# Layer 1: the store of the upper four chunks of image 13 as nine accesses of every ninth partition

## The chip, the cores and the metric

The kernel runs on one core of one Trainium2 chip. The metric is the time of one execution on the device in microseconds (us); the median of several runs counts. Names used below: PE is TensorE, DVE is VectorE, ACT is ScalarE, POOL is GpSimd, SP is SyncE, the engine that issues most DMAs here. A core has sixteen DMA engines. "Landing" is the moment at which the last of the sixteen marks of a DMA has been counted on its semaphore.

## The reference

Input and output are 16 images of 128 channels by 64 by 64, float32. Layer 0 adds to `x` a diagonal LSTM of its group-normalised self; layer 1 adds a small simulated quantum circuit, again of the group-normalised input. Cut to what matters:

```python
def _L0_conv_ref(x, w_is, b_is, w_ss, b_ss):      # skewed rows, a scan over 127 columns
    i_s = einsum('oi,bihw->bohw', w_is, skew(x)) + b_is
    def step(carry, ist):
        gates = ist + w_ss[:, :, 0] @ shifted(h) + w_ss[:, :, 1] @ h + b_ss
        c_new = f * c + i * g
        h_new = o * tanh(c_new)
    return unskew(hs)

def _L1_conv_ref(x, pre_w, pre_b, q_weights, post_w, post_b):
    xq = x.transpose(0, 2, 3, 1).reshape(-1, C) @ pre_w.T + pre_b
    z = _simulate(xq, q_weights)                  # 4 qubits, 2 layers
    out = z @ post_w.T + post_b
    return out.reshape(N, H, W, -1).transpose(0, 3, 1, 2)

x = x + _L0_conv_ref(_gn(x), ...)
x = x + _L1_conv_ref(_gn(x), ...)
```

## The kernel before, in words

The 128 channels lie on the 128 partitions. The whole activation is kept on the chip as far as it fits: the tile `ring` holds 40 of the 64 image rows of all 16 images; the other 24 rows of each image, `low`, lie in DRAM.

Three stages follow each other. Stage one loads `x`, takes its statistics and prepares weights (to about 90 us). Stage two is the scan, a chain of steps on PE, DVE, ACT and POOL (to about 1276 us); it hardly uses DMAs. Stage three is layer 1, and the change lies at its end.

In stage three an image is cut into eight chunks of 512 positions (`CHUNK`), `k` = 0 to 7. Chunks 0 to 2 come from `low` by way of small tiles (`spare`, `trio`, `low`), loaded by POOL's queue (`load`, `low_rows`); chunks 3 to 7 are read in `ring`. For each image: `angles` (line 1099, PE) makes the angles, `sines` (ACT, DVE) their sines, `squares` (line 1129, PE, then ACT) the amplitudes, `outputs` (line 1149, PE) the values, and `finish` adds them to the image on DVE, one instruction for each chunk (line 1167), and issues the store (line 1173) on SP. The loop at the end runs over images 1 to 15 and works them in order; an order written out by hand overlaps neighbours (all inside `tc.manual_schedule()`).

How the stores are cut: `together(b, k)` tells how many chunks go into one store. Chunks 0 to 3 go out singly, 256 KB each: a row of 2 KB on each of 128 partitions. Of chunks 4 to 7, images 1 to 3 make two stores of 512 KB, images 4 to 14 one store of 1 MB (a row of 8 KB on each partition), issued when chunk 7 is done. Image 15, the last, stores all its chunks singly. So images 4 to 14 have five stores each, image 15 has eight.

The order on SP is the order of the program. Each DMA that SP issues takes the next of eight semaphores in turn, and first waits until the DMA that used that semaphore before, eight places earlier, has landed. It waits for DVE's instruction of its chunk as well. At most eight of SP's stores are so under way at any time. The end of the program (line 1290) waits until every store has landed.

Of the kernel before, what the change touches and what calls it, by code (L numbers as in the profile page):

```python
# [17 lines left out]
NB = 16  # L18
# [13 lines left out]
FEW = 96  # L32
TWICE = 128
LEAST = 128
AHEAD = RING - SLOTS
BAND = NW + 1
NSTEP = BAND + NW + SLOTS - 1
# [45 lines left out]
def kernel(  # L83
# [16 lines left out]
    nc = tc.nc  # L100
# [38 lines left out]
    def place(r):  # L139

        return (r + AHEAD if r < SLOTS else r - SLOTS) * NW

# [21 lines left out]
    with ExitStack() as scan:  # L164
# [55 lines left out]
        def above(v, a, b):  # L220

            v = v[:, 1, 0:1]
            dims = [list(v.ap[0]), [NB - NC, 2], [1, b - a]]
            return bass.AP(v.tensor, v.offset + a - NB, dims)
# [8 lines left out]
        with ExitStack() as prep:  # L233
# [25 lines left out]
            def rows(b):  # L259
                half = SLOTS // 2  # L260
                first = 0 if b else AHEAD
                early = ((first, half - first), (half, half))
                for r, n in (*(early if b < 3 else ((0, SLOTS),)), (SLOTS, AHEAD)):
                    nc.sync.dma_start(
# [6 lines left out]
            def behind(b):  # L271
# [10 lines left out]
                out=qw, in_=q_weights.rearrange("l w a -> (l w a)").partition_broadcast(P)  # L282
            )
            nc.sync.dma_start(out=ring[:, 0, place(0) : place(AHEAD)], in_=xv[0, :, 0 : AHEAD * NW])
            for i in range(2):
# [146 lines left out]
            def cleared():  # L432
                for v in (*hst, *xns, none, cst[:, :, 0:LEAST]):
                    nc.gpsimd.memset(v, 0.0)
                    yield
                nc.gpsimd.memset(eps, EPS)
                nc.gpsimd.tensor_sub(apart_of, ident, group)
                yield
                nc.gpsimd.memset(w_image, 0.0)
                yield  # L440
# [60 lines left out]
            for g in ORDER:  # L501
                first[g] = ps_gate.tile([P, 2, NC], F32, name=f"ps0_{g}", tag="gate")
                for w, rhs in ((w1T, hst[0][:, :, 0 : LEAST // 2]), (w0T, above(hst[0], 0, LEAST // 2))):
                    nc.tensor.matmul(
                        first[g][:, :, 0 : LEAST // 2],
                        lhsT=w[:, g * 128 : (g + 1) * 128],
# [106 lines left out]
        def reach(t):  # L613

            b = columns(t)[1]
            return b + 4 if b < NC else b

        def plain(t):
            a, b = columns(t)
            return b - a <= FEW  # L620
# [5 lines left out]

        def wide(t, least=LEAST):

            a, b = columns(t)[0], reach(t)
            return max(0, min(a, b - least)), max(b, min(NC, a + least))  # L630

        def diagonal(t, band, q, j0, j1):


            r = 2 * j0 + q + AHEAD * (1 - band)
            at = r * NW + t - BAND * band - 2 * j0 - q
# [15 lines left out]
        def apart(op, *groups):  # L652

            for key in groups:
                tc.declare_no_dep(op.ins, group=key, reason="other rows of the ring")
            return op

        def ahead_of(op, band, j1):

            apart(op, "stores", *(f"reload{g}" for g in reloads if band == 0 or 2 * j1 <= AHEAD + 4 * g))  # L660

# [24 lines left out]
        def gate_ps(t):  # L686

            a, b = wide(t, LEAST // 2)
            ps = {} if t else first
# [172 lines left out]
        def step(t, ps):  # L862

            a, b = columns(t)
            few = plain(t)
            a0, b0 = wide(t, LEAST // 2 if few else LEAST)
            w = reach(t)
# [209 lines left out]
    def rows_of(b, k):  # L1077
        if k < NT:
            return lows[NT * b + k]
        at = place(2 * ROWS * k)  # L1080
        return ring[:, b, at : at + CHUNK]

    def half(v, c):

        if c is None:
            return v
        return v[:, c * BLOCK : (c + 1) * BLOCK]
# [71 lines left out]
    def finish(b, h, po, c=None):  # L1159
        for j in range(4):  # L1160
            k = 4 * h + j
            v = rows_of(b, k)
            x1, y, o = half(v, c), po[j], ov[b, :, k * CHUNK : (k + 1) * CHUNK]
            to = v
            if c is not None:
                o, to = o[:, c * BLOCK : (c + 1) * BLOCK], x1
            nc.vector.scalar_tensor_tensor(to, y, b_out, x1, ALU.add, ALU.add)  # L1167
            n = together(b, k) if c is None else 1
            if (k + 1) % n == 0:
                if n > 1:  # L1170
                    at = place(2 * ROWS * (k + 1 - n))
                    o, to = (u[:, at0 : at0 + n * CHUNK] for u, at0 in ((ov[b], (k + 1 - n) * CHUNK), (ring[:, b], at)))
                nc.sync.dma_start(out=o, in_=to)
            if c is None or c == 1 and k < NT:
                places.append(v)

    def together(b, k):

        if k < 4 or b == NB - 1:
            return 1  # L1180
        return 2 if b < 4 else 4
# [8 lines left out]
    with tc.manual_schedule():  # L1190
# [15 lines left out]
        angles(1, 1, th, (1,))  # L1206
        ths[1, None] = th
        finish(0, 0, po, 0)
        squares(0, 1)
        po = outputs(0, 1, 0)  # L1210
        finish(0, 1, po, 0)
        later = sines(1)
        next(later)
        po = outputs(0, 0, 1, (0, 1))
        th = angles(2, parts=(0,))
        po += outputs(0, 0, 1, (2, 3))
        finish(0, 0, po, 1)
        next(later, None)
        po = outputs(0, 1, 1, (0,))
# [74 lines left out]
```

## Time and profile before

| | us |
|---|---|
| median of 3 runs (lowest, highest) | 1399.43 (1399.15, 1399.73) |
| the profiled execution's own time | 1399.66 |
| its span, first to last instruction | 1397.8 |

The stages, by windows of the profile (busy us in each):

| window, us | PE | DVE | ACT | POOL | DMA share | GB/s |
|---|---|---|---|---|---|---|
| 0 to 88, loads and statistics | 68.25 | 76.01 | 60.23 | 27.12 | 0.98 | 392 |
| 88 to 1276, the scan | 1174.74 | 795.28 | 685.97 | 840.14 | 0.07 | 24 |
| 1276 to 1397.8, layer 1 | 108.03 | 102.30 | 40.09 | 25.39 | 0.93 | 360 |
| of it 1345 to 1387 | 39.59 | 40.74 | 12.41 | 0.00 | 1.03 | 412 |
| of it 1387 to 1397.8 | 0.00 | 0.00 | 0.00 | 0.00 | 0.59 | 227 |

How to read it: the DMA share is the mean busy share of the sixteen DMA engines (a little over 1 where packets overlap). The stores of layer 1 in the profile's list of issues, with size and median time from issue to landing:

```profile
out_dram<-ring SPq DMA_DIRECT2D x11, 1024.0 KB, 9.1
out_dram<-ring SPq DMA_DIRECT2D x37, 256.0 KB, 7.2
out_dram<-low SPq DMA_DIRECT2D x14, 256.0 KB, 9.1
```

SP's stream is shown in rows of its own (SPq): start, duration, line, what is stored, and how many in a row. The first of the eleven stores of 1 MB is image 4's, the tenth image 13's, the eleventh image 14's.

### The profile page before, as it was taken

To read this page: it belongs to the slowest core of one execution; us is meant where nothing else is said; L and a number is where in the kernel's file an instruction comes from. 1 tells how busy PE (TensorE), PEld (TensorE's weight loads), DVE (VectorE), ACT (ScalarE), POOL (GpSimd) and SP (SyncE) were. 2 spreads that over 40 slices of the span, in tenths; PEclk is the share of its full clock that TensorE was granted. 3 is DMA by queue.
4 is the path that set the end of the run, shared out by engine and by line. 5 is a ranking of instruction groups with operands and counts; after the bars stand their busy time and mean duration, and the time that the engine had idled before them with its cause. 6 is when DMAs were issued, how large, how long until landed. Compare 5 with 4: busy or idle time off the path is not lost. (4 is left out here: it accounts for less than half of the span.)

```text
span 1397.8 us, 19939 instructions
## 1 busy us (share of the span) xinstructions
PE 1351.0 (97%) x6058; PEld 966.6 (69%) x6058; DVE 973.6 (70%) x2520; ACT 786.3 (56%) x1881; POOL 892.6 (64%) x1584
## 2 busy tenths in 40 slices
PE   7789999999999999999999999999999999989996
PEld 6668887777777777767777767777777778886332
DVE  6973565577767775677777776666665566876996
ACT  6765666555555555555555555555555566644331
POOL 3236777766677777777777766777777667764400
PEclk9999999999999999999999999999999999999998
DMA  9940000000000000133333100000000000014998
GB/s 373 417 199 1 2 1 1 1 1 1 1 1 1 1 1 1 60 121 121 121 121 120 61 1 1 1 1 0 1 1 1 1 0 1 1 31 144 382 415 354
DMA packets 52746, 107.02 MB, mean 77 GB/s; under 512 B 3824, under 2 KB 31504, under 8 KB 49568
## 3 DMA queue, kind: packets, MB, share of 16 engines
q1 hardware_dynamic: 49024, 95.17, 18.3%
q0 software_dynamic: 3472, 10.58, 2.0%
q8 instruction: 48, 0.79, 0.2%
q14 instruction: 58, 0.48, 0.1%
q10 hardware_dynamic: 144, 0.01, 0.0%
HBM read 59.61 MB, written 46.14 MB: 76 GB/s over the span
## 5 line engine op out<-in xcount | busy, mean ns | idle before, releaser
L693 PE MATMUL ps<-spare,wxT 128*128 128x512 f32 (+18 forms) x1280 | 479.6, 518 | 0.6 <-POOL spare L684 0.6
L887 DVE TENSOR_TENSOR ps<-ps,both 128x256 f32<-128x256 f32 (+9 forms) x536 | 219.8, 410 | 295.5 <-PE ps L872 291.1
L891 ACT ACTIVATE ps<-ps,bias 128x512 f32<-128x512 f32 (+23 forms) x480 | 279.2, 583 | 219.5 <-DVE ps L887 183.1
L693 PEld LDWEIGHTS ps<-spare,wxT 128*128 128x128 f32 x1280 | 230.9, 190 | 173.2 <-issue 155.5
L872 PE MATMUL ps<-trio,w1T 128*128 128x256 f32 (+14 forms) x1088 | 306.3, 363 | 0.0
L872 PE MATMUL ps<-trio,w0T 128*128 128x256 f32 (+14 forms) x1088 | 305.5, 362 | 0.0
L922 ACT COPY both<-ps 128x256 f32<-128x256 f32 (+9 forms) x536 | 189.6, 356 | 181.0 <-PE ps L872 161.5
L872 PEld LDWEIGHTS ps<-spare,wsT 128*128 128x128 f32 x1088 | 196.0, 190 | 78.8 <-DVE spare L957 30.4
L872 PE MATMUL ps<-spare,wsT 128*128 128x256 f32 (+14 forms) x1088 | 243.6, 365 | 1.6 <-DVE spare L957 1.3
L730 POOL TENSOR_TENSOR ring<-ring,spare 128x256 f32<-128x256 f32 (+15 forms) x375 | 231.4, 643 | 18.3 <-DVE spare L957 18.0
L872 PEld LDWEIGHTS ps<-trio,w1T 128*128 128x128 f32 x1088 | 201.6, 190 | 22.3
L872 PEld LDWEIGHTS ps<-trio,w0T 128*128 128x128 f32 x1088 | 201.1, 190 | 21.2
L684 POOL TENSOR_TENSOR spare<-spare,rstd 128x512 f32<-128x512 f32 (+10 forms) x160 | 170.9, 1068 | 14.2 <-DVE rstd L528 1.7
L678 POOL TENSOR_TENSOR spare<-ring 128x256 f32<-128x256 f32 (+13 forms) x165 | 139.4, 845 | 0.0
L951 ACT ACTIVATE g<-cst 128x256 f32<-128x256 f32 (+20 forms) x320 | 103.0, 368 | 64.2 <-DVE cst L950 63.6
L957 DVE TENSOR_TENSOR spare<-g,ps 128x256 f32<-128x256 f32 (+17 forms) x319 | 105.3, 367 | 44.3 <-ACT g L951 39.4
L720 POOL TENSOR_TENSOR trio<-spare 128x240 f32<-128x240 f32 (+9 forms) x136 | 102.5, 754 | 36.7 <-DVE spare L957 33.1
L672 POOL TENSOR_TENSOR spare<-ring,mean 128x256 f32<-128x256 f32 (+15 forms) x191 | 122.5, 641 | 2.5 <-DVE mean L517 2.0
L891 ACT ACTIVATE g<-ps,bias 128x512 f32<-128x512 f32 (+20 forms) x160 | 97.3, 608 | 27.6 <-DVE ps L887 21.3
L950 DVE TENSOR_TENSOR cst<-cst,ps 128x256 f32<-128x256 f32 (+20 forms) x320 | 104.5, 368 | 5.5
L947 DVE TENSOR_TENSOR ps<-ps,g 128x512 f32<-128x512 f32 (+20 forms) x160 | 95.1, 594 | 18.7 <-ACT g L891 18.5
L939 DVE TENSOR_TENSOR cst<-cst,ps 128x512 f32<-128x512 f32 (+20 forms) x160 | 92.7, 579 | 16.5 <-POOL spare L231 10.9
(385 smaller groups left out, 1172.3 us busy)
## 6 DMA issues: line engine op xcount, KB each, us to landing
ring<-in_x_dram SPq DMA_DIRECT2D x13, 1024.0 KB, 9.8
low<-ring SPq DMA_DIRECT2D x6, 2048.0 KB, 7.6
ring<-in_x_dram SPq DMA_DIRECT2D x6, 2048.0 KB, 8.2
out_dram<-ring SPq DMA_DIRECT2D x11, 1024.0 KB, 9.1
out_dram<-ring SPq DMA_DIRECT2D x37, 256.0 KB, 7.2
trio<-in_x_dram SPq DMA_DIRECT2D x7, 768.0 KB, 7.6
rest<-in_x_dram SPq DMA_DIRECT2D x7, 768.0 KB, 7.8
ring<-in_x_dram SPq DMA_DIRECT2D x18, 256.0 KB, 9.9
```

Source lines behind the costliest of these rows:

```text
L672: op = nc.gpsimd.tensor_sub(by_pairs(xn, 0, j0, j1), x0, over(mean1, j1 - j0))
L678: op = nc.gpsimd.tensor_sub(by_pairs(xn, 1, j0, j1), lower, of)
L684: nc.gpsimd.tensor_mul(v, v, r)
L693: nc.tensor.matmul(ps[g][:, :, a:b], lhsT=wxT[:, g * 128 : (g + 1) * 128], rhs=xns[t % 2][:, :, a:b], start=t > 0, stop=True, skip_group_c ...
L730: op = engine.tensor_add(x1, x1, by_pairs(new, q, j0, j1))
L872: nc.tensor.matmul(out, lhsT=w[:, g * 128 : (g + 1) * 128], rhs=rhs, start=False, stop=True, skip_group_check=True,)
L887: nc.vector.tensor_add(v, v, both[g][:, a:b])
L891: nc.scalar.activation(to[:, :, a:w], ps[g][:, :, a:w], FUNC[g], bias=bias[:, g : g + 1])
L922: nc.scalar.copy(both[g][:, a:b], ps[g][:, 0, a:b])
L950: nc.vector.tensor_add(c[:, q], c[:, q], ig[:, q])
L951: nc.scalar.activation(th[:, q, a:w], c[:, q], AF.Tanh)
L957: nc.vector.tensor_mul(new[:, q, a:v], th[:, q, a:v], act[GO][:, q, a:v])
```

## The change

In `finish`, when the store of several chunks of image 13 (`b == NB - 3`) is due, it is issued as nine DMAs in place of one. DMA number p takes the partitions p, p + 9, p + 18 and so on: 15 partitions for p = 0 and 1, 14 for p = 2 to 8, each with its whole row of 8 KB. All the nine are issued one after another on SP. All other stores are as before; what is computed is the same.

```diff
@@ -32,6 +32,7 @@
 LEAST = 128
+APART = 9
 AHEAD = RING - SLOTS
@@ -1170,7 +1171,9 @@
                     o, to = (u[:, at0 : at0 + n * CHUNK] for u, at0 in ((ov[b], (k + 1 - n) * CHUNK), (ring[:, b], at)))
-                nc.sync.dma_start(out=o, in_=to)
+                apart = APART if n > 1 and b == NB - 3 else 1
+                for p in range(apart):
+                    nc.sync.dma_start(out=o[p::apart], in_=to[p::apart])
             if c is None or c == 1 and k < NT:
                 places.append(v)
```

The program built from it has eight more DMAs on SP, 15 or 14 rows of 2048 floats each, and nothing else differs in any engine's order. The nine take semaphores 4 to 8, 1, 2, 3 and 4 of the turn of eight (counting from image 15's last store as 1), so the ninth waits for the first; the stores behind them use the same semaphores as before.

## The prediction

> **What bounds the kernel now.** I read the last stage from its end backwards, since the edit touches only image 13's store. First, the chain of waits, whose last pieces are work of VectorE at line 1167, and SyncE's waits from 1330 us on; the second line is the only wait after the last store.
>
> ```profile
> 1382.01 2.72 DVE ring L1167 x4
> 1385.39 1.32 DVE ring L1167 x2
> SPq L1290 <- DMA out_dram<-ring: 4.6, 1, 4.6
> ```
>
> The last computation ends at 1385.39 + 1.32 = 1386.71 us, yet the span goes on to 1397.8: the last 11.1 us belong to the stores alone. SyncE stands 4.6 us at the end until the last one has landed (1396.50 by the trace's landing marks), and 1.3 us of closing work follows. Next, the stage cut into windows (length; then busy time of PE, weight loads, DVE, ACT, POOL with counts; granted clock; DMA share; GB/s).
>
> ```profile
> 1384.00:1386.00 2.00, 0.59 (x2) 0.00 (x0) 2.00 (x5) 0.00 (x0) 0.00 (x0) 0.76 1.06 419
> 1390.00:1392.00 2.00, 0.00 (x0) 0.00 (x0) 0.00 (x0) 0.00 (x0) 0.00 (x0) 0.50 1.04 392
> 1392.00:1394.00 2.00, 0.00 (x0) 0.00 (x0) 0.00 (x0) 0.00 (x0) 0.00 (x0) 0.50 0.58 221
> 1394.00:1396.00 2.00, 0.00 (x0) 0.00 (x0) 0.00 (x0) 0.00 (x0) 0.00 (x0) 0.50 0.07 26
> ```
>
> Until 1392 the sixteen DMA engines are full. From 1394 to 1396 the share is 0.07, about one sixteenth: one engine works alone. The landing marks (sixteen for each store) say the same: of the last store, fifteen lie between 1393.35 and 1394.38, the sixteenth at 1396.50. That one engine trails in every store of the stage: 0.93 us behind the next at the store landing 1349.86, 2.07 at 1381.23, 2.12 at the end. It alone sets the end. Last, how SyncE issues.
>
> ```profile
> 1283.02 1.30 SPq L1173 DMA_DIRECT2D out_dram<-trio  x3
> 1284.41 2.38 SPq L1173 DMA_DIRECT2D out_dram<-ring  x5
> ...
> 1377.07 1.98 SPq L1173 DMA_DIRECT2D out_dram<-ring  x2
> 1379.14 3.06 SPq L1173 DMA_DIRECT2D out_dram<-low  x3
> 1382.29 1.11 SPq L1173 DMA_DIRECT2D out_dram<-ring  x1
> 1383.49 8.36 SPq L1173 DMA_DIRECT2D out_dram<-ring  x9
> ```
>
> Against an idle queue (first two rows) eight stores start within 3.4 us, one each 0.48 us, taking 0.33 to 0.41. Late ones take 0.33 to 1.2. The second store of the 1377.07 row, at 1378.23, is the edited one; image 14's first follows at 1379.14. Each store takes the next of eight semaphores and first waits until the store eight places before it has landed.
>
> **The change, part by part.** *Removed:* one access of 128 rows of 8 KB. The trace's packets are whole rows (8192 bytes, median 309 ns), eight to an engine: 8 × 0.309 = 2.47 us; the trailing engine's marks for this store stand 2.53 apart (1383.85, 1386.38). *Added:* nine accesses of 15, 15, and seven times 14 rows, 116 KB each on average; 8 more issues on SyncE with 8 more semaphore waits. VectorE's, ScalarE's and TensorE's streams are unchanged, and nothing there waits for a store so late. Bytes are unchanged.
>
> *Which engines carry them.* No row shows a store of fewer than 16 rows. Since a packet is a whole row, 14 rows reach at most 14 engines. Two ends for the trailing engine, then: it gets no row and drops 2.53 us, or one of each piece, 9 × 0.31 = 2.79, so 0.26 us more. I take the first, because each piece leaves an engine out. The Trainium skill ("DMA: Bandwidth & Descriptors", section on why a DMA increments its semaphore by 16) has the split use the largest number up to 16 that divides the slowest dimension, on the lowest-numbered engines: 14 or 15, never the last. Its table of latencies calls engines 7 and 15 usually slower; no view here numbers the trailing one, so the page leaves both ends open too.
>
> *What the nine waits cost.* Nine issues move every later store eight places on, a full turn, so those keep their semaphores. The pieces meet landings of stores already under way, which the edit can't hasten. Pieces 1 to 3 find theirs landed (1377.37, 1378.00, 1378.71). Piece 4 needs the store of 1372.44, image 12's large one: 1381.23. Pieces 5 to 8 need 1381.91, 1382.54, 1383.21, 1383.85. Piece 9 needs piece 1, which lands near 1382. So piece 8 starts at 1383.85 + 0.07 = 1383.92. With 0.33 to 0.43 for an issue and 0.09 between issues, image 14's first store starts two issues later, at 1384.76 to 1384.96, against 1379.14: 5.7 us later. Behind it in SyncE's queue stand image 14's other four stores and image 15's eight, whose data is ready by 1386.71.
>
> *What is late next.* The trailing engine ends its last row of image 13's other stores at 1383.85 − 0.39 = 1383.46 (0.39 us lie between the last packet's end, 1396.11, and its mark, 1396.50). From issue to first packet are 0.84 us (1283.02 to 1283.86 at the idle queue), so it starts again at 1385.60 to 1385.80, idle for 2.2 us. Then it has images 14 and 15, which took it 1396.11 − 1385.99 = 10.12 us before. The faster engines, all but dry too by then, start beside it. While all were full around 1350 to 1376 the trailing one took some 0.66 us for a 256 KB store and 2.63 for a large one, so 12 × 0.66 + 2.63 = 10.55 bounds it from above. End: 1385.60 + 10.12 + 0.39 = 1396.11 to 1385.80 + 10.55 + 0.39 = 1396.74. I take 1396.4: against 1396.50, **0.1 us less**. The 2.53 us saved are spent on 2.2 us of standing dry and on company. The cover that keeps the later issues free is the queue of that engine; image 15's last store waits for image 14's large one, at 1385.7 + 5.2 + 0.4 = 1391.3, while its queue reaches to 1395, so it isn't late.
>
> [...] Eight stores of 128 KB, issued 0.48 us apart, each landed 1.7 to 1.8 us after its issue: the fixed part overlaps, and nine pieces cost issues, not landings. [...]
>
> *Sum.* The profiled execution took 1399.66 us with a span of 1397.84; the median of the runs is 1399.43, 0.23 less. 1399.43 − 0.1 = **1399.3**.
>
> **Rivals.** (a) *The trailing engine carries a row of each piece.* It doesn't run dry: 1383.46 + 2.79 = 1386.25, then 10.12 to 10.55 and 0.39: 1396.8 to 1397.2, +0.3 to +0.7, so 1399.9. For it: nothing in the trace names the engine. Against: two of sixteen are left out.
>
> (b) *Relief without starving.* If the waits for landings don't hold the pieces back, the next-slowest engine sets the end: 1394.38 + 0.31 for its ninth row = 1394.7, −1.8, so 1397.6. Against: of the stores from 1365 on, eight start within 0.07 us of the landing of the one eight places before (1391.45 and 1391.52 the last). It's also the floor: no reading reaches −2.8 us.
>
> (c) *Slower: the pieces issue at the late price.* The rows from 1366 to 1391 hold 25 stores in 25.2 us, about 1.0 us each, though 0.33 at 1391.52, and I can't tell from them what stretches an issue. With c for one issue and its gap, image 14's first store starts at the later of 1383.92 + 2c and 1381.30 + 6c: the second decides above c = 0.66. At 1.0 it is 1387.3, 2.4 us past my value: +2.3, so 1401.7. If the twelve issues behind also keep 1.0, the last starts at 1399.3 and lands 0.84 + 0.65 + 0.39 later, 1401.2: +4.7, so 1404.1. For it: the late rows; against: the idle-queue rows, and the queue is nearly empty here.
>
> (d) *The split isn't one row to an engine.* All on one engine: 128 × 0.309 = 39.6 us there, in place of 2.5: about +37, so 1436. Against: every row of 128 spreads evenly; for it: nothing but the lack of a row.
>
> **How the numbers follow.** Mine 0.56; (a) 0.20; (b) 0.08; (c) 0.13; (d) 0.03. What a measurement of this kernel can tell from no change is about 0.2%, 2.8 us. Mine, (a), (b) and the mild form of (c) lie within it; the full form and (d) are slower. Half of (c) and a mishap in the same place beside (d) make slower 0.13; same 0.85; faster 0.02, for something no row shows. Likeliest alone: 1399.0 to 1399.8 by its bounds and the runs' own spread. The 8-in-10 range takes in (a), half of (b)'s way and the mild (c): 1398.5 to 1402.0.
>
> **What would show it.** After: nine issues at line 1176, the fourth starting at 1381.3 and the eighth near 1383.9; image 14's first store at 1384.8; a window between 1382 and 1386 with a DMA share well under 1; the end without a stretch of 0.07, all engines stopping together near 1396. If the stretch at 0.07 stays, (a) holds. If the share stays at 1 and the landing comes near 1394.7, (b). If pieces take 0.6 us or more, (c). A TensorE or VectorE row that moves before 1378 would make the whole reading wrong.

## The result, and the profile after

The changed kernel takes 1401.58 us (median of 15 runs, 1400.82 to 1407.14) against 1399.60 us before (15 runs, 1398.21 to 1400.54): a ratio of 1.0019, 95% interval 1.0011 to 1.0027, so 1.5 to 3.8 us slower. The range on record held the time; the forecast of 0.1 us less did not hold, since the interval is clear of 1. I had also said that a measurement of this kernel can't tell less than about 0.2%; that was too coarse: fifteen runs told 0.19%.

The profiled execution took 1401.83 us. The page of the changed kernel, its first line and the line on packets:

```profile
span 1400.1 us, 19947 instructions
DMA packets 52858, 107.02 MB, mean 76 GB/s; under 512 B 3936, under 2 KB 31616, under 8 KB 49680
```

The span is 2.2 us longer, with the same bytes. Of packets under 512 bytes, almost all of them the semaphore marks with which each engine ends its share of a DMA, there are 112 more than before (3936 against 3824). That tells how many engines the pieces use: nine accesses of 15, 15 and seven times 14 marks make 128, in place of the 16 of one access. So the change does what it says. The computation hardly moved. The end of the chain of waits after the change:

```profile
1382.28 2.72 DVE ring L1168 x4
1385.65 1.32 DVE ring L1168 x2
```

Its last piece ends at 1386.97, against 1386.71. The loss lies behind it. The windows of the end after the change, to be read like those before (the last three columns: granted clock, DMA share, GB/s):

```profile
1380.00:1382.00 2.00, 2.00 (x12) 0.68 (x10) 1.24 (x3) 0.00 (x0) 0.00 (x0) 1.00 0.48 187
1382.00:1384.00 2.00, 2.00 (x7) 0.85 (x6) 2.00 (x4) 0.00 (x0) 0.00 (x0) 1.00 0.49 198
1384.00:1386.00 2.00, 0.86 (x3) 0.03 (x1) 2.00 (x4) 0.00 (x0) 0.00 (x0) 0.85 0.32 127
1386.00:1388.00 2.00, 0.00 (x0) 0.00 (x0) 0.97 (x2) 0.00 (x0) 0.00 (x0) 0.50 0.54 209
1394.00:1396.00 2.00, 0.00 (x0) 0.00 (x0) 0.00 (x0) 0.00 (x0) 0.00 (x0) 0.50 1.01 382
```

The windows of that stretch before, where the prediction doesn't show them:

```profile
1380.00:1382.00 2.00, 2.00 (x11) 0.68 (x10) 1.24 (x2) 0.00 (x0) 0.00 (x0) 1.00 1.03 419
1382.00:1384.00 2.00, 2.00 (x6) 0.88 (x6) 2.00 (x5) 0.00 (x0) 0.00 (x0) 1.00 0.99 389
1386.00:1388.00 2.00, 0.00 (x0) 0.00 (x0) 0.70 (x2) 0.00 (x0) 0.00 (x0) 0.50 0.99 402
```

After the change there is a trough of 8 us, in which the sixteen engines are on average under half busy (0.46), where before they were full; and the window 1394 to 1396, in which one engine worked alone before (0.07), is now full (1.01). All sixteen marks of the last store lie between 1398.56 and 1398.71. The trailing engine no longer ends alone, because all of them had run dry and began on image 14's stores together: the sixteen marks of the first lie between 1388.50 and 1388.72. SyncE's stream, and under it the durations (ns: shortest, median, longest) of the seven pieces of 14 rows:

```profile
1379.41 6.99 SPq L1176 DMA_DIRECT2D out_dram<-ring  x8
1386.51 1.43 SPq L1176 DMA_DIRECT2D out_dram<-low  x3
...
L1176 SPq DMA_DIRECT2D out_dram<-ring x7: 771/775/784, 1380.7 to 1385.6; - x7
```

The first row holds pieces 2 to 9. Each of the seven takes about 0.775 us, with little spread, though the queue runs empty under them. (Pieces 1 and 2, issued while the engines were still full, took 1.16 and 1.25 us.) Image 14's first store starts at 1386.51, not at 1384.8.

For what follows a measure is needed that the small shifts of the earlier stages don't reach. I take the landing of image 13's fourth store, which is issued ahead of the edit in every run (below: "the mark"), and measure from there to the last landing ("the distance"): 12.65 us before (1383.85 to 1396.50), 14.62 after (1384.10 to 1398.71). Each is from one profile. The run of the issue prices below (e5) leaves this stage as before and has 12.71, and two profiles of one kernel lie 0.06 to 0.28 us apart, so differences under 0.3 us say nothing. All the runs together:

| run | image 14's first store starts, from that landing | to the last landing | ratio to before (95%) |
|---|---|---|---|
| before | -4.71 | 12.65 | |
| the change | +2.41 | 14.62 | 1.0019 (1.0011 to 1.0027) |
| the change again (e0) | +2.31 | 14.53 | 1.0017 (1.0008 to 1.0026) |
| eight of every eighth (e1) | +0.61 | 13.16 | 1.0003 (0.9995 to 1.0012) |
| nine of neighbours (e2) | +0.88 | 13.81 | 1.0011 (1.0002 to 1.0021) |
| nine of neighbours again | +1.08 | 14.09 | 1.0010 (1.0001 to 1.0019) |
| pieces by ScalarE (e4) | -4.76 | 13.43 | 1.0008 (0.9999 to 1.0017) |
| pieces by SyncE, same order (e4b) | -5.43 | 15.20 | 1.0020 (1.0012 to 1.0029) |
| 112, 7, 7 and 2 rows (e6) | -0.86 | 13.03 | 0.9999 (0.9990 to 1.0008) |
| hollow, every ninth (e7) | +1.94 | 16.07 | 1.0028 (1.0016 to 1.0040) |
| hollow, neighbours (e7b) | +0.89 | 15.04 | 1.0018 (1.0009 to 1.0027) |

### The profile page after: what moved, and what is told of

Read it like the earlier page. It is cut to its first block, busy times and chain, and to the rows that moved or that the text cites. A ratio compares the mean times of both kernels' runs of the same rounds, so it can differ in the third digit from the quotient of the medians.

```text
span 1400.1 us, 19947 instructions
## 1 busy us (share of the span) xinstructions
PE 1351.3 (97%) x6058; PEld 966.7 (69%) x6058; DVE 974.0 (70%) x2520; ACT 786.3 (56%) x1881; POOL 893.0 (64%) x1584
## 2 busy tenths in 40 slices
DMA packets 52858, 107.02 MB, mean 76 GB/s; under 512 B 3936, under 2 KB 31616, under 8 KB 49680
```

## The experiments

Three theories were in play. S: an access that leaves engines out costs SyncE some 0.8 us to issue. P: the stride over partitions does. W: neither, but the semaphore waits, or small accesses as such.

**Eight pieces of 16 rows (e1).**

```diff
-APART = 9
+APART = 8
```

> Image 13's store as eight accesses of every eighth partition: 16 rows each, one for every DMA engine. Theory S (an access that leaves engines out holds SyncE about 0.78 us per issue, against 0.33 to 0.43 for one that uses all sixteen): each piece takes 0.33 to 0.43 us, the eighth starts near 1383.9 to 1384.0, image 14's first store at 1384.3 to 1384.5, the trailing engine finds its work in time, span 1397.8 +- 0.4, ratio 1.0000 +- 0.0005. Rival W (many small accesses and their semaphore waits cost the same whatever their number of rows): pieces of 0.78 us again, image 14's first store at 1385.6 or later, span over 1399, ratio 1.0010 or more.

```profile
L1176 SPq DMA_DIRECT2D out_dram<-ring x5: 493/493/510, 1380.5 to 1383.2; - x5
```

These are pieces 4 to 8 in SyncE's stream: 0.49 us, between S's 0.33 to 0.43 and W's 0.78. Image 14's first store started 0.61 us after the mark, 1.8 us sooner than in the changed kernel, and the loss in distance shrank from 1.97 to 0.51 us. The ratio can't be told from 1; its interval reaches to 1.0012 and so holds W's 1.0010 as well, and it is the price and the distance that speak against W. But an issue of sixteen rows wasn't as cheap as S said.

**Nine pieces of neighbouring partitions (e2, twice).**

```diff
-                apart = APART if n > 1 and b == NB - 3 else 1
-                for p in range(apart):
-                    nc.sync.dma_start(out=o[p::apart], in_=to[p::apart])
+                cuts = (0, 15, 30, 44, 58, 72, 86, 100, 114, P) if n > 1 and b == NB - 3 else (0, P)
+                for p0, p1 in zip(cuts, cuts[1:]):
+                    nc.sync.dma_start(out=o[p0:p1], in_=to[p0:p1])
```

> Nine accesses again of 15, 15 and seven times 14 rows, but of neighbouring partitions in place of every ninth. Theory S: pieces of 0.77 to 0.79 us as in the changed kernel, image 14's first store at 1386.5, span 1400.1 +- 0.5, ratio 1.0015 to 1.0025. Rival P (the stride of nine partitions is what costs): pieces of 0.33 to 0.43 us, image 14's first store near 1384.9, span near 1398.2, ratio under 1.0006.

> The nine accesses of neighbouring partitions again, on the same chip as the changed kernel. Theory P: pieces of 0.32 to 0.38 us, span 1398.6 +- 0.5, ratio 1.0003 to 1.0010, at least 0.0008 under that of the changed kernel. Rival S: ratio as for the changed kernel.

The same numbers of rows, but no stride. The last four pieces (the five ahead of them took 0.38 to 1.16 us):

```profile
L1176 SPq DMA_DIRECT2D out_dram<-ring x4: 318/328/383, 1382.2 to 1383.9; - x4
```

Here S falls: 14 rows cost 0.33 us. P's price holds, but not the time it gave: 1.0011 and 1.0010, about half the loss of the change, where I had expected under 1.0006 at first. The windows of the first of these runs show why:

```profile
1382.00:1384.00 2.00, 2.00 (x6) 0.58 (x4) 2.00 (x4) 0.00 (x0) 0.00 (x0) 1.00 0.75 216
1384.00:1386.00 2.00, 1.15 (x4) 0.29 (x2) 2.00 (x4) 0.00 (x0) 0.00 (x0) 0.99 0.85 189
```

The engines are 75 to 85% busy and still move only about 200 GB/s. The 128 packets of 8 KB of the pieces take longer: median 0.51 us (0.53 in the second run), a tenth of them over 0.93, against 0.32 us in the changed kernel and 0.31 before. So the stride of nine spares the transfers something that neighbouring partitions pay, and pays for it in issues. That they pay it without any load too is seen in the run of the issue prices below: there 14 rows of 2 KB from neighbouring partitions (with the stride on the DRAM side) took 0.08 to 0.25 us each, 14 rows of every ninth partition 0.08 to 0.09. The Trainium skill ("DMA: Bandwidth & Descriptors", section "The descriptor swizzle") shows, for a transfer that writes 128 partitions, four neighbouring partitions behind one port. Counted by its formula, with one port to an engine, up to four rows of a piece share a port where the partitions are neighbours, two where every eighth is taken, one where every ninth is; the medians of 0.51, 0.46 and 0.32 us go in that order. This fits, but the pieces of the runs differ in more than that, and no view shows a port. In the second run two early pieces took 1.28 and 1.08 us as well, and the gap to the changed kernel, sent along on the same chip, came out as 0.0007 rather than the 0.0008 or more that I had expected; the intervals can't tell the two apart.

> The changed kernel itself, for comparison on the same chip: span 1400.1 +- 0.5, ratio 1.0014 to 1.0024, pieces of 0.77 to 0.79 us.

The changed kernel repeated itself (1.0017, span 1400.4, distance 14.53).

**The pieces off SyncE (e4), and a control (e4b).** The nine pieces are issued behind ScalarE's last work, or at the same place of the program by SyncE. `finish` puts image 13's large store aside (`later_stores`) for it. SyncE's other stores keep their order in both. The semaphores are not the same, though I had expected so: on SyncE the nine follow each other in the turn of eight, on ScalarE they are mixed with stores of images 14 and 15.

```diff
+    def pieces_by(queue):
+        for o, to in later_stores:
+            for p in range(APART):
+                queue.dma_start(out=o[p::APART], in_=to[p::APART])
...
             if b + 1 < NB:
                 squares(b + 1)
+            if b == NB - 2:
+                pieces_by(nc.scalar)      # e4b: nc.sync
```

> The nine pieces are issued by ScalarE behind its last work, squares of image 15, so that SyncE's stream holds image 14's first four stores at the place where the pieces stood. Theory S: the pieces keep a price near 0.8 us but on ScalarE, which has nothing left to do; image 14's first store starts near 1378.3, no window before 1392 has a DMA share much under 1, and the trailing engine with its ninth row sets the end: span 1398.1 to 1398.6, ratio 1.0002 to 1.0006. Rival W (the waits for landings or the small transfers themselves cost it): the end stays near that of the changed kernel, span 1400, ratio 1.0015 or more.

> The same order of stores and the same semaphores as in the run with ScalarE, but the nine pieces issued by SyncE, behind image 14's first four stores. Theory S: nine times 0.82 us stand before image 14's large store, which starts near 1389.5; span 1399.5 to 1400.3, ratio 1.0012 to 1.0020, over a microsecond more than with ScalarE. Rival W: the same time as with ScalarE, since waits and transfers are the same.

With ScalarE: SyncE's stream, the durations of the pieces, and the last windows.

```profile
1378.80 2.15 SPq L1177 DMA_DIRECT2D out_dram<-low  x3
1381.05 4.95 SPq L1177 DMA_DIRECT2D out_dram<-ring  x4
...
L1186 ACTq DMA_DIRECT2D out_dram<-ring x9: 785/795/1534, 1381.7 to 1394.8; - x9
...
1392.00:1394.00 2.00, 0.00 (x0) 0.00 (x0) 0.00 (x0) 0.00 (x0) 0.00 (x0) 0.50 0.90 323
1394.00:1396.00 2.00, 0.00 (x0) 0.00 (x0) 0.00 (x0) 0.00 (x0) 0.00 (x0) 0.50 0.39 157
1396.00:1398.00 2.00, 0.00 (x0) 0.00 (x0) 0.00 (x0) 0.00 (x0) 0.00 (x0) 0.50 0.14 57
```

With SyncE: the pieces from the second on, and image 14's large store.

```profile
L1186 SPq DMA_DIRECT2D out_dram<-ring x8: 771/776/813, 1383.3 to 1389.1; - x8
...
1389.97 0.47 SPq L1177 DMA_DIRECT2D out_dram<-ring  x1
```

The price is about the same on either engine, 0.78 to 0.80 us. On ScalarE, which has nothing left to do, it costs much less: image 14's large store starts at 1382.97 and the distance is 13.43. On SyncE that store starts at 1389.97 and the distance is 15.20. The 1.77 us between them are what it costs that the pieces stand in the one queue that feeds the end, where they hold it for 7.6 us (1382.28 to 1389.87); the medians differ by the same 1.8 us (1400.49, 1402.33). The waits, which differ too, don't make that up: on SyncE no piece from the second on waited for a landing, they start 0.82 to 0.86 us apart. The span with SyncE, 1400.8, is 0.5 us over what I had expected. With ScalarE 0.8 us of loss remain in distance (ratio 1.0008; its interval, 0.9999 to 1.0017, holds S's ratio and W's alike).

What those 0.8 us are the marks on the semaphores show in part, and it is not what I had expected. SyncE's last store landed at 1395.11. The end, 1396.99, is that of the last piece, which ScalarE issued at 1394.78: pieces 5 and 6 had waited for stores of image 15 (landed 1390.92 and 1391.89), and the rest followed at their price or a little more. All fourteen marks of that piece lie between 1396.86 and 1396.99. So it is the issues, now on ScalarE, that set the end of this run, and not the trailing engine, whose mark of the piece before came at 1396.36.

**The price by itself (e5).** The kernel before, with 48 small stores at the start of the scan, where SyncE idles; one run. The DMA engines idle only from about 90 us on: their share is 0.94 from 88 to 90 us, the end of stage one's loads, 0.18 from 90 to 92 and 0.08 from 92 to 94.

```diff
+            if t == 20:
+                for n, (rows, to) in enumerate(PRICED):
+                    nc.sync.dma_start(out=scratch[n, to], in_=wxT[rows])
```

> The kernel before, with 48 extra stores on SyncE in the scan (at t = 20, where SyncE and the DMA engines are idle), rows of 2 KB of the weight tile wxT into a scratch tensor: 14 sorts, three of each, then 14 rows with the stride on one side only. Theory P (the stride over partitions sets the price of an issue, not the number of rows or engines): neighbouring 128, 126, 16, 14 and 7 rows all take 0.33 to 0.43 us, every ninth partition 0.75 to 0.80 whether 14 or 15 rows, every eighth near 0.5 whether 16 or 14 rows. Rival S (engines left out set it): 126, 14 and 7 rows and 14 rows of every eighth cost 0.7 or more, 16 and 128 rows 0.4 with any stride. Rival L (only a loaded queue stretches an issue): all sorts take 0.33 to 0.43 us here. With the stride on one side only, P expects the price to follow one of the sides.

In this order: 14 neighbours; 126 neighbours; 14 rows of every ninth; 14 of every eighth; 16 of every eighth; 14 of every other; 14 with the stride of nine on the tile's side only; on the DRAM side only (ns: shortest, median, longest).

```profile
L980 SPq DMA_DIRECT2D scratch<-wxT x3: 307/336/499, 88.5 to 89.6; - x3
L980 SPq DMA_DIRECT2D scratch<-wxT x2: 399/408/418, 103.9 to 104.3; - x2
L980 SPq DMA_DIRECT2D scratch<-wxT x3: 743/747/872, 90.2 to 91.9; - x3
L980 SPq DMA_DIRECT2D scratch<-wxT x3: 748/778/787, 97.0 to 98.7; - x3
L980 SPq DMA_DIRECT2D scratch<-wxT x2: 582/584/587, 95.8 to 96.4; - x2
L980 SPq DMA_DIRECT2D scratch<-wxT x3: 748/769/777, 106.6 to 108.3; - x3
L980 SPq DMA_DIRECT2D scratch<-wxT x2: 747/753/759, 113.4 to 114.2; - x2
L980 SPq DMA_DIRECT2D scratch<-wxT x2: 382/382/382, 115.6 to 116.1; - x2
```

A row that counts two leaves out the first of its three: 0.57 us for 126 neighbours, 0.56 for 16 of every eighth, 0.77 with the stride on the tile's side, 0.55 with it on the DRAM side.

L falls: the prices stand without any load. P and S are each half right. A stride over the tile's partitions makes an issue dearer, whatever the stride is (2, 3, 4, 7, 8 and 9 were tried); with a stride, 16, 32 or 64 rows cost 0.54 to 0.60 us, 14 or 15 rows 0.74 to 0.79 (once 0.87). Without one, 7, 14, 126 and 128 rows cost 0.29 to 0.43, but for the first of a sort, which took up to 0.57; the three of 16 rows, issued while the engines were still full, took 0.90, 0.57 and 0.42. Why, no run shows.

**Which engine trails (e6).**

```diff
+                cuts = (0, 112, 119, 126, P) if n > 1 and b == NB - 3 else (0, P)
```

> Image 13's store as four accesses of neighbouring partitions: 112 rows, then 7, 7 and 2. If an access of 7 rows uses seven engines and the trailing engine is none of them, its marks end together and the trailing engine has seven rows in place of eight: the end 0.3 us earlier, span 1397.2 to 1397.8, ratio 0.9995 to 1.0000. If the trailing engine is one of the seven, it has nine or ten rows: one mark of a 7-row piece lies 1 us or more behind the others, and the span is 1398.1 to 1398.6.

Of the first 7-row piece, six marks came between 1384.21 and 1385.48, and the seventh at 1387.04, 1.56 us behind. So the trailing engine is one of the seven that such a piece uses. The distance (13.03, 0.4 more) fits the row that it has on top. The times decide nothing: the span of the profile, 1398.7, is the longest of eleven with a median of 1397.6, which lies in the band that I had given to the other case, and the ratio is 0.9999. The pieces of 14 rows in the changed kernel say the same: the last of their marks followed each other at 1385.06, 1385.37, 1385.70, 1386.01 and 1386.31, one row of 0.31 us at a time; the first of them is 1.57 us behind the next, the last 0.13.

**The issues and waits without the transfers (e7, e7b).** Image 13's store stays whole; ahead of it go eight extra accesses of 64 bytes a row. The eight leave every other store's semaphore as it was.

```diff
+                for p in range(8 if n > 1 and b == NB - 3 else 0):
+                    rows = slice(p, P, 9)      # e7b: slice(14 * p, 14 * p + 14)
+                    nc.sync.dma_start(out=scratch[p, rows], in_=w_out[rows, 0:16])
                 nc.sync.dma_start(out=o, in_=to)
```

> The kernel before with image 13's store whole, and ahead of it eight extra accesses of every ninth partition (15 or 14 rows) of 64 bytes each into a scratch tensor: the issues and the semaphore waits of the pieces almost without their transfers. From the landing of image 13's fourth store to the last landing, 12.65 us before and 14.62 in the changed kernel. Theory P (the price of a strided issue holds SyncE): issues of 0.75 to 0.80 us, image 13's store near 1385.6, the engines dry for 3 us, the distance 15.4 to 16.0, ratio 1.0017 to 1.0027. Rival W (the waits alone): the same distance as with neighbouring partitions.

> The same eight extra accesses with 14 neighbouring partitions each. Theory P: issues of 0.31 to 0.43 us, so that only the waits for landings are left: the eighth near 1383.9, image 13's store near 1384.4, the engines dry for 1.7 us, the distance 14.2 to 14.8, 1.0 to 1.5 us less than with every ninth partition, ratio 1.0009 to 1.0017.

Every ninth partition, then neighbours; under each a window in the trough.

```profile
L1176 SPq DMA_DIRECT2D scratch<-w_out x8: 747/748/1247, 1377.8 to 1384.1; - x8
...
1382.00:1384.00 2.00, 2.00 (x8) 0.61 (x5) 1.96 (x3) 0.00 (x0) 0.00 (x0) 1.00 0.07 18
```

```profile
L1176 SPq DMA_DIRECT2D scratch<-w_out x8: 306/307/1187, 1377.7 to 1383.2; - x8
...
1382.00:1384.00 2.00, 2.00 (x6) 0.58 (x4) 2.00 (x4) 0.00 (x0) 0.00 (x0) 1.00 0.06 13
```

Both dry the engines out (0.07 and 0.06), and both lose: 3.4 and 2.4 us in distance, a little over what I had expected of each, though image 13's store started sooner than expected (1384.94 and 1383.61). Their difference, 1.03 us, is the price of the stride. The 2.4 us of the neighbours are almost wholly the cost of the waits for landings: eight places of the turn, filled with accesses that carry almost nothing. The eighth started at 1383.20, right behind the landing that it waited for (1383.18), and took 0.31 us. So W was right that waits cost, and wrong that they cost alike. (The medians, 1403.02 and 1401.75, lie 1.3 us apart; the intervals overlap.)

## Why the prediction was wrong, point by point

- *What bounds the end* held: the stores alone, one trailing engine before, and the turn of eight semaphores. Nothing ahead of the edit moved by more than 0.3 us.
- *The waits for landings* held: piece 4 started at 1381.53, right behind the landing that I had named (1381.45; forecast 1381.23). That the queue would run dry held too.
- *"With 0.33 to 0.43 for an issue"* is the step that failed. A piece took 0.775 us and 0.04 to the next. That is the slower rival (c), with c = 0.82: 1381.53 + 6 × 0.82 = 1386.45, measured 1386.51. That (c)'s 1401.7 comes so near to the measured 1401.58 is in part luck: its c of 1.0, taken from rows whose spacing holds waits for landings too, puts six issues 1.1 us too late, and what the end took on top (below) makes up for most of that. The cause that I gave it, late load, was not the one: the price goes with the stride over partitions and, given a stride, with a number of rows that isn't a multiple of sixteen. I had taken the nearest row, the 128-row stores at an idle queue, which have neither. From the mark, image 14's first store came at +2.41 rather than +1.01 (1384.86 - 1383.85): 1.4 us.
- *"I take the first"*, that the trailing engine carries no row of the pieces, failed as well: rival (a) was right there. The relief of 2.53 us on which my sum rested never came. In the changed kernel this cost no time of its own, since the trailing engine too ran dry and waited for SyncE. By piece 8 its mark came with the others' (1386.87 to 1386.98). What the ninth row costs where the issues don't hold it up can only be estimated, from e4: its mark of the eighth piece came at 1396.36, and one row of 0.31 us more makes 1396.67, a distance of 13.11, 0.46 us more than before and within (a)'s 0.3 to 0.7. The rest of e4's 0.78 us is the issue of the last piece.
- *From image 14's first store to the end* I had 11.5 us (1396.4 - 1384.86) and it took 12.2 in both profiles of the changed kernel: its landing came 2.2 us after the issue (1.9 forecast), and a 256 KB store at the end took 0.68 us where all engines run in step. That is the other 0.7 us: 1.4 + 0.7 - 0.1 = 2.0, the 1.97 measured in distance.
- The signs that I had named read rightly: the share in the trough, a 0.07 that is gone, pieces of 0.6 us or more for (c).
- The Trainium skill's rule for few engines ("DMA: Bandwidth & Descriptors", section "Why a DMA increments its semaphore by 16 and not by 1"), by which 14 rows go to 14 engines, agrees with the 112 extra marks; that these are the lowest-numbered ones, no view shows. The same page's "Rules for kernel authors", which for bandwidth want 128 partitions and at least 1 MiB in a DMA, were right in sign here.

## What to carry to other kernels

Where one queue feeds saturated DMA engines, count the issues as work: nine accesses in place of one used up the room of eight stores in flight, and 7 us of issuing, while the engines needed 2.5 us for the bytes. Look up the price of an issue in a row of the same shape, the stride over partitions and the number of rows among it, and not only in one of the same size; if there is none, the wide bound belongs in the likeliest case too. To relieve a slow DMA engine, find out first whether the access that is meant to leave it out does.

## What the runs showed of the hardware

A stride over the tile's partitions more than doubles an issue's time for 14 rows (medians of 0.75 to 0.78 against 0.31 to 0.34 us) on SyncE, loaded or idle, and it takes 0.80 on ScalarE; a stride on the DRAM side alone costs little (0.38). Accesses of few neighbouring partitions have slower packets (8 KB in 0.51 to 0.53 us, median) than those of every ninth (0.32); every eighth took 0.46. None of the versions ran faster than the kernel before.
